# Layer 0's softmax reciprocals: taken of four gathered rows, and spread from HBM with one load per head pair

## The chip, the cores and the metric

The kernel runs on one NeuronCore of a Trainium2 chip. The metric is device time in microseconds (us) from start to end of the program, the median of several runs. A profile of one execution is used beside it. The engines are named as in the profile: PE is TensorE (matmuls), PEld its weight loads, DVE is VectorE, ACT is ScalarE, POOL is GpSimd, SP is SyncE, which here issues nearly all DMAs.

## What is computed

Eight samples of 512 channels by 1024 positions (32x32), float32, pass through two attention layers with residuals. Layer 0 is the one that the change touches:

```python
# layer 0, per sample: group norm over 32 groups, then 8 heads of 64 channels
qkv = einsum('oc,bchw->bohw', qkv_w, h) + qkv_b
attn = softmax(einsum('bhnd,bhmd->bhnm', q, k) / sqrt(64), axis=-1)
o    = einsum('bhnm,bhmd->bhnd', attn, v)
x    = x + einsum('oc,bchw->bohw', proj_w, o) + proj_b
```

Layer 1 has one sample-wide norm and a single head of 512 channels. Softmax is evaluated without subtracting a maximum: exponentials are summed, and the sum's reciprocal is applied after the product with v, to o rather than to the probabilities. For each query position and head, one reciprocal is therefore needed: 8 heads x 1024 positions per sample.

## The kernel before

**Work and stages.** The samples are taken in turn. For each, layer 0 (`layer0`) makes v, then q and k of the odd head pairs, and then runs a loop over 64 attention units; q and k of the even pairs were made ahead. A unit is (pair, g, kt): a pair of heads, a half g of the queries (512 of them), and one of eight blocks of 128 keys. The pairs come in the order 0, 2, 1, 3. For a unit, PE computes the scores (L921) into one of two PSUM buffers, ACT takes the exponential (L778) into a tile `p`, DVE adds `p` to the pair's running sum `acc` (L780, not for kt = 0), and two units later PE multiplies `p` with v (L940) into one of two other PSUM buffers. After the last kt, ACT (L946) and DVE (L947) move the result out to the output tile `os`, and so free that buffer.

**Order.** PE, ACT and DVE run in the order in which the program text issues their work. In the loop, `couple_steps(i)` places the work on sums so many units after the end of a pair; in the following stage a table `hooks` places it after so many steps of the products that make the next sample's q and k (L612, with evacuations at L425, L642, L644). SP issues its DMAs in program order too, each after the waits ahead of it. SBUF tiles come from a pool of 36 tiles of 128x1024; a new tile's first writer waits for the last users of the tile that had the place before. The two PSUM pools "s" and "o" have two buffers each.

**The sums.** When both halves of a pair are done, three DMAs (`fold`, L1039 to L1041) and one DVE addition (`folded`, L1046) bring its two accumulators into one tile. Two pairs make a couple: pairs 0 and 2, then pairs 1 and 3. Ones-matmuls (`sum_couple`, L1054) then write the sums of the couple's four heads into two banks, one per query half, each head's row repeated over 32 partitions. `copy_couple` (L1063, through `held`, L788) copies a bank to an `inv` tile of 128x512. `one_over_couple` (L1066) takes the reciprocal of that whole tile in place and issues eight DMAs (L1072), each copying 32 rows of a head to 32 partitions of the tile `spreads[pair]`, two copies for each head's 64 channels. `held_couple` (L1078) makes ACT read the reciprocals once, for a check on their size. `divide_couple` (L1081, through `divide`, L960) multiplies `os` by the spread reciprocals.

**Where this stands.** The first couple is handled inside the loop, while the units of pairs 1 and 3 run (7 to 18 units after the end of pair 2). The second couple is handled in the stage after the loop, between the products for the next sample's q and k. Right after that stage comes layer 0's projection (`project`, L612 with tiles `ps_p`), whose operands are `os[0][0]` and `os[1][0]` first, then the differences `t_p` made by `combine2` (L1010), and whose PSUM results DVE evacuates at L1183. Its second chunk of channels in each operand belongs to pairs 1 and 3. The last sample (b = 7) has a path of its own (L1116 to L1131) that the change leaves alone, so the couples occur 14 times, twice in each of 7 samples.

**Layer 1.** `sums` (L1550) already does something like the changed code, once a sample: a reciprocal of a 128x256 tile, a store of its four distinct rows to HBM (L1562), and one load that broadcasts the 4 KB row to all 128 partitions (L1564), with this source:

```python
rows.rearrange("n q -> (n q)").unsqueeze(0).to_broadcast([P, 8 * P])
```

Of the kernel before, what the change touches and what calls it, by code (L numbers as in the profile page):

```python
# [37 lines left out]
FP = mybir.dt.float32  # L38
# [8 lines left out]
P = 128  # L47
C = 512
NC = C // P
N = 1024  # L50
NT = N // P
HALF = 512
HD = 64
# [12 lines left out]
def two_attention_blocks(  # L66
# [17 lines left out]
    nc = tc.nc  # L84
    B = x.shape[0]

    const = ctx.enter_context(tc.tile_pool(name="const", bufs=1))
    tpool = ctx.enter_context(tc.tile_pool(name="t", bufs=36))
    wpool = ctx.enter_context(tc.tile_pool(name="w", bufs=3))
    dram = ctx.enter_context(tc.tile_pool(name="dram", bufs=1, space=bass.MemoryType.DRAM))  # L90
    upool = ctx.enter_context(tc.tile_pool(name="u", bufs=5))
    onepool = ctx.enter_context(tc.tile_pool(name="one", bufs=1))
    accpool = ctx.enter_context(tc.tile_pool(name="acc", bufs=2))
# [4 lines left out]
    def banks(tag, name):  # L98
        return psum.tile([P, 2, HALF], FP, tag=tag, name=name)

    def tile2(name):
        return tpool.tile([P, 2, HALF], FP, tag="t", name=name)
# [8 lines left out]
    def piece(ts, cc, half):  # L111

        return ts[cc // 2][half][:, cc % 2, :]
# [52 lines left out]
    ones = const.tile([P, P], FP, tag="ones", name="ones")  # L166
    nc.gpsimd.memset(ones, 1.0)

    extent = const.tile([P, B * 10 + 2], FP, tag="extent", name="extent")
    extents = iter(range(extent.shape[1]))  # L170


# [90 lines left out]
    def next_weight():  # L263

        w = waiting.pop(0)
        if coming:
            name = coming.pop(0)
            waiting.append(Weight(name) if name in stored else load_first(name))
        return w
# [12 lines left out]
    def room(name, n=-1):  # L282

        return spares[n] if spares else banks("s", f"ps_{name}")[:, 0, :]
# [302 lines left out]
    def together(*groups):  # L587

        groups = list(groups)
        spares.clear()  # L590
        while groups:
            for g in list(groups):
                if next(g, g) is g:
                    groups.remove(g)
                else:
                    yield
        spares.clear()

    def at_steps(steps, hooks):

        n = -1
        for n, _ in enumerate(steps):
            for hook in hooks.get(n, []):
                hook()
        assert n >= max(hooks, default=-1)
# [177 lines left out]
    def held(value, name, to=None):  # L783

        if to is None:
            to = onepool.tile([P, HALF], FP, tag="held", name=f"held_{name}")[:, : value.shape[1]]
        n = next(extents)
        nc.scalar.activation(to, value, AF.Identity, accum_out=extent[:, n : n + 1])  # L788
# [20 lines left out]
    def flat(t):  # L809
        return t.rearrange("p h n -> p (h n)")  # L810

    def pairs_qk(w, oc, bs, qs, ks, b):

        for ts, n, bias, name in [(qs, 0, V_BQ0, "q"), (ks, 1, V_BK0, "k")]:
            for i in (oc, oc + 2):
                t = tile2(f"{name}_0_{b}_{i}")
                ts[i] = [t[:, half, :] for half in range(2)]
            yield make_channels(
                w.parts[n], 0, oc, bs, vec[:, bias : bias + NC],
                lambda chunk, half, ts=ts: ts[chunk][half], f"{name}_0_{b}",  # L820
            )
# [65 lines left out]
    def layer0(bs, qs, ks, b, norm_next):  # L887
# [24 lines left out]
        accs, sums, invs, spreads = {}, {}, {}, {}  # L912
# [45 lines left out]
        def divide(pair, g, inv):  # L958
            part = piece(os, pair, g)
            nc.vector.tensor_tensor(part, part, inv, ALU.mult)  # L960
# [45 lines left out]
        def combine2(n, k):  # L1006
            x, y = {
                1: (os[0][1], os[0][0]), 2: (comb["B22"], comb["T1"]), 3: (comb["B22"], os[0][1]), 4: (comb["B21"], comb["T2"])
            }[n]
            nc.vector.tensor_tensor(comb[f"T{n}"][:, k, :], x[:, k, :], y[:, k, :], ALU.subtract)  # L1010
# [21 lines left out]
        couples, folds, ps_couple = [ORDER[:2], ORDER[2:]], {}, []  # L1032

        def fold(pair):


            (a, c), t = (accs[pair, g] for g in range(2)), tile2(f"fold_{b}_{pair}")
            low, high = slice(0, HD), slice(HD, P)
            nc.sync.dma_start(t[low], a[high])  # L1039
            nc.sync.dma_start(t[high], c[low])  # L1040
            nc.sync.dma_start(a[high], c[high])  # L1041
            folds[pair] = t

        def folded(pair):
            a = accs[pair, 0]
            nc.vector.tensor_tensor(a, a, folds.pop(pair), ALU.add)  # L1046

        def sum_couple(couple, banks_of):


            for n, (pair, j) in enumerate((pair, j) for pair in couple for j in range(2)):
                for g, bank in enumerate(banks_of):
                    rows = slice(g * HD, (g + 1) * HD)
                    nc.tensor.matmul(  # L1054
                        bank[n * 32 : (n + 1) * 32, :], ones[rows, :32], accs[pair, 0][rows, j, :],
                        start=True, stop=True,
                    )
            ps_couple[:] = banks_of

        def copy_couple(couple, g):  # L1060
            name = f"{b}_{couple[0]}_{g}"
            invs[g] = accpool.tile([P, HALF], FP, tag="inv", name=f"inv_{name}")
            held(ps_couple[g], f"sum_{name}", invs[g])  # L1063

        def one_over_couple(couple, g):
            nc.vector.reciprocal(invs[g], invs[g])  # L1066
            for n, pair in enumerate(couple):
                if g == 0:
                    spreads[pair] = tile2(f"inv_{b}_{pair}")
                for j in range(2):  # L1070
                    for r in range(2):
                        nc.sync.dma_start(  # L1072
                            spreads[pair][(j * 2 + r) * 32 : (j * 2 + r + 1) * 32, g, :],
                            invs[g][(n * 2 + j) * 32 : (n * 2 + j + 1) * 32, :],
                        )

        def held_couple(g):
            held(invs.pop(g), f"inv_{b}_{g}")  # L1078

        def divide_couple(couple, g):  # L1080
            for pair in couple:  # L1081
                divide(pair, g, spreads[pair][:, g, :])

        def ended(i):

            pair, g, kt = units[i] if 0 <= i < len(units) else (None, None, None)
            return pair if (g, kt) == (1, NT - 1) else None

        def couple_steps(i):
            if ended(i - 1) is not None:  # L1090
                fold(ended(i - 1))
            if ended(i - 5) is not None:
                folded(ended(i - 5))
            couple = couples[0]
            if ended(i - 7) == couple[1]:
                ps_sum = banks("o", f"ps_sum_{b}_{couple[0]}")
                sum_couple(couple, [ps_sum[:, g, :] for g in range(2)])
            for g, (at_copy, at_over, at_held, at_divide) in enumerate([(7, 8, 14, 13), (8, 10, 18, 15)]):
                if ended(i - at_copy) == couple[1]:
                    copy_couple(couple, g)  # L1100
                if ended(i - at_over) == couple[1]:
                    one_over_couple(couple, g)
                if ended(i - at_held) == couple[1]:
                    held_couple(g)
                if ended(i - at_divide) == couple[1]:
                    divide_couple(couple, g)

        last = norm_next is None
        for i in range(2, len(units) + 2):
# [6 lines left out]
            pair, g, kt = units[i - 5] if i >= 5 else (None, None, None)  # L1116
            name = f"0_{b}_{pair}_{g}"
# [8 lines left out]
            pair, g, kt = units[i - 9] if i >= 9 else (None, None, None)  # L1126
            if pair in invs and kt == NT - 1:
                held(invs.pop(pair), f"inv_0_{b}_{pair}_{g}")
            pair, g, kt = units[i - 10] if i >= 10 else (None, None, None)
# [3 lines left out]
        if b == 0:  # L1133
            rows, = throughs
# [3 lines left out]
        if not last:  # L1138


            couple = couples[1]
            hooks = {
                0: [lambda n=n: combine2(n, 0) for n in range(1, 5)],
                1: [lambda: folded(end)],
                3: [
                    lambda: sum_couple(couple, [room("sum", g) for g in range(2)]),
                    lambda: copy_couple(couple, 0), lambda: copy_couple(couple, 1),
                    lambda: one_over_couple(couple, 0),
                ],
                5: [lambda: held_couple(0)],  # L1150
                6: [lambda: one_over_couple(couple, 1)],
                7: [lambda: divide_couple(couple, 0)],
                8: [lambda: held_couple(1)],
                9: [lambda: divide_couple(couple, 1)] + [lambda n=n: combine2(n, 1) for n in range(1, 5)],
            }
            at_steps(
                together(*pairs_qk(next_weight(), 0, combine.parts, qs_next, ks_next, b + 1)), hooks
            )
# [1011 lines left out]
```

## Time and profile before

| | us |
|---|---|
| three runs: median (lowest to highest) | 2839.69 (2839.13 to 2842.56) |
| profiled execution: span, first to last instruction | 2838.1 |
| PE busy, share of the span | 2825.0 (100%) |
| DVE busy | 2124.3 (75%) |
| ACT busy | 1118.0 (39%) |
| DVE reciprocals of 128x512 (L1066), 28 of them | 93.7 |
| DMAs that spread them (L1072), 224 of them, issue to landing each | 2.0 |

The profiled execution's own time is its span of 2838.1 us; the median of the runs is 1.6 us more. Busy times are unions of an engine's instructions. The ends of matmuls are modelled, so that a PE at 100% is not proof that no time is lost; waits are better seen in the distance from one matmul's start to the next one's. In the timeline lines, the first column is the start in us, the second the time from the first start to the last end of a merged row, then engine, line, operation, output and inputs, shapes, the number of instructions, and in brackets the idle time before it with what ended it.

### The profile page before, as it was taken

How to read it: one execution, taken by the hardware profiler on the slowest of the kernel's cores; microseconds unless marked ns; L12 is line 12 of the kernel's file. 1: busy time of each engine (PE TensorE's matmuls, PEld its weight loads, DVE VectorE, ACT ScalarE, POOL GpSimd, SP SyncE). 2: the span in 40 equal slices, each digit the busy share in tenths (PEclk: the TensorE clock that was granted, in tenths of full speed). 3: DMA queues.
4: the chain of work that ended last, by engine and by line, in shares of the span. 5: the costliest groups of instructions: out<-in, count | busy, mean ns of one | idle time of the engine just before them, and what ended most of it. 6: DMA issues, size and time to landing. Idle time of an engine off the chain costs nothing.

```text
span 2838.1 us, 38370 instructions
## 1 busy us (share of the span) xinstructions
PE 2825.0 (100%) x15328; PEld 1518.4 (53%) x15328; DVE 2124.3 (75%) x2891; ACT 1118.0 (39%) x1564; POOL 273.6 (10%) x236
## 2 busy tenths in 40 slices
PE   9999999999999999999999999999999999999999
PEld 5434765347643476435773356733567335673365
DVE  6686696867867678777777777777777777767867
ACT  3462324623256232553325522265232642326432
POOL 0000220003100040000400004000040000400011
PEclk9999999999999999999999999999999999999999
DMA  8512132121322213213132131322213222121001
GB/s 289 179 42 74 58 121 94 42 89 53 111 93 50 86 70 107 80 46 108 56 108 79 40 106 56 108 79 46 100 59 105 79 56 90 63 85 57 8 16 39
DMA packets 81227, 228.90 MB, mean 81 GB/s; under 512 B 20080, under 2 KB 20880, under 8 KB 74640
## 3 DMA queue, kind: packets, MB, share of 16 engines
q1 hardware_dynamic: 76576, 210.61, 23.0%
q10 hardware_dynamic: 4464, 15.76, 1.7%
q8 instruction: 122, 2.00, 0.3%
q14 instruction: 65, 0.53, 0.1%
HBM read 157.35 MB, written 30.70 MB: 66 GB/s over the span
## 4 chain that ended last, share of the span: by engine, by line
PE 91%; DVE 6%; issue 1%; SPq 1%; DMA 0%; ACT 0%; POOL 0%; DVEq 0%; POOLq 0%
PE s L921 16%; PE ps_o L940 15%; PE ps_q L612 10%; PE ps_v L627 7%; PE ps_o L1489 7%; PE ps_p L612 5%; PE ps_l L1325 4%; PE ps_s L1308 4%; PE ps_k L612 3%; PE ps_l_v L627 3%; PE ps_s L1325 3%; PE ps_l_qk L849 3%; PE ps_s_v L870 2%; PE ps_s_two L1619 2%; PE ps_s_qk L842 2%; PE ps_o_v L870 1%
## 5 line engine op out<-in xcount | busy, mean ns | idle before, releaser
L778 ACT ACTIVATE p<-s 128x1024 f32<-128x1024 f32 x512 | 524.0, 1025 | 322.1 <-PE s L921 308.3
L780 DVE TENSOR_TENSOR acc<-acc,p 128x1024 f32<-128x1024 f32 x384 | 469.2, 1222 | 99.4 <-ACT p L778 86.3
L940 PE MATMUL ps_o<-p,v 64*64 64x512 f32 x4096 | 528.6, 589 | 0.0
L940 PEld LDWEIGHTS ps_o<-p,v 64*64 64x64 f32 x4096 | 156.6, 133 | 282.8 <-issue 278.9
L921 PE MATMUL s<-q,k 64*64 64x512 f32 x2304 | 298.5, 591 | 0.0
L921 PE MATMUL s<-c_q,c_k 64*64 64x512 f32 x1792 | 233.0, 590 | 0.0
L339 POOL TENSOR_TENSOR rstd<-rstd,minus_half 128x4 f32<-128x4 f32 (+1 forms) x16 | 19.8, 1239 | 2087.7 <-DVE rstd L338 2087.7
L921 PEld LDWEIGHTS s<-q,k 64*64 64x64 f32 x2304 | 86.3, 133 | 162.6 <-issue 156.6
L1489 PE MATMUL ps_o<-t_p,s_v 128*128 128x512 f32 x384 | 168.2, 594 | 0.0
L921 PEld LDWEIGHTS s<-c_q,c_k 64*64 64x64 f32 x1792 | 67.7, 133 | 126.3 <-issue 114.9
L780 DVE TENSOR_TENSOR acc<-p,p 128x1024 f32<-128x1024 f32 x64 | 77.9, 1217 | 73.5 <-ACT p L778 73.5
L1299 ACT ACTIVATE p<-p,factor 128x512 f32<-128x512 f32 (+1 forms) x112 | 85.3, 780 | 115.7 <-DVE p L1335 91.2
L1313 ACT COPY p<-ps_s 128x512 f32<-128x512 f32 x96 | 53.1, 588 | 177.1 <-PE ps_s L1308 177.1
L1489 PEld LDWEIGHTS ps_o<-t_p,s_v 128*128 128x128 f32 x384 | 72.3, 190 | 91.3 <-issue 89.2
L1335 DVE TENSOR_TENSOR p<-ps_l,p 128x512 f32<-128x512 f32 x136 | 90.0, 683 | 41.0 <-PE ps_l L1325 40.7
L612 PE MATMUL ps_p<-t_p,w_p 128*128 128x512 f32 x256 | 114.8, 597 | 2.4 <-DVE u_p L1183 1.3
L612 PE MATMUL ps_q<-t,w_wqk 128*128 128x512 f32 x256 | 116.0, 597 | 0.0
L425 ACT COPY u_q<-ps_q 128x512 f32<-128x512 f32 x75 | 43.6, 581 | 177.1 <-PE ps_q L612 177.1
L1066 DVE RECIPROCAL inv<-inv 128x512 f32<-128x512 f32 x28 | 93.7, 3346 | 22.9 <-ACT inv L788 22.9
L425 ACT COPY u_v<-ps_v 128x512 f32<-128x512 f32 x48 | 28.1, 586 | 204.9 <-PE ps_v L627 185.9
L1335 DVE TENSOR_TENSOR p<-ps_s,p 128x512 f32<-128x512 f32 x112 | 74.8, 684 | 37.9 <-PE ps_s L1325 37.9
L627 PE MATMUL ps_v<-w_v,t_again 128*128 128x256 f32 x448 | 99.0, 379 | 0.0
(457 smaller groups left out, 4903.5 us busy)
## 6 DMA issues: line engine op xcount, KB each, us to landing
x<-in_x SPq DMA_DIRECT2D x92, 512.0 KB, 6.8
w_qk<-stored_qk SPq DMA_DIRECT2D x14, 1792.0 KB, 7.3
inv<-inv SPq DMA_DIRECT2D x248, 64.0 KB, 2.0
w_wqk<-stored_wqk SPq DMA_DIRECT2D x8, 1792.0 KB, 7.6
fold<-acc SPq DMA_DIRECT2D x56, 256.0 KB, 3.1
w_wvo<-stored_wvo SPq DMA_DIRECT2D x8, 1792.0 KB, 7.5
out<-x SPq DMA_DIRECT2D x28, 512.0 KB, 3.3
w_v<-stored_v SPq DMA_DIRECT2D x7, 1792.0 KB, 7.1
```

What stands on the lines that cost most here:

```text
L612: nc.tensor.matmul(bank, w[a][:, k, c * P : (c + 1) * P], bs[b][:, k, :], start=fresh and k == 0, stop=k == 1, skip_group_check=True,)
L627: nc.tensor.matmul(bank[:, u * 2 * P : (u + 1) * 2 * P], bs[b][:, k, n * P : (n + 1) * P], w[a][:, k, :], start=fresh and u == k == 0, sto ...
L778: nc.scalar.activation(p, s, AF.Exp, scale=factor)
L780: nc.vector.tensor_tensor(acc, first, p, ALU.add)
L921: nc.tensor.matmul(s[cols, j, :], ks[pair][k0 // HALF][rows, k0 % HALF : k0 % HALF + HD], qs[pair][g][rows, :], start=True, stop=True,)
L940: nc.tensor.matmul(o[cols, half, :], vs[kt][rows, c0 : c0 + HD], p[rows, j, :], start=kt == 0, stop=kt == NT - 1,)
L1066: nc.vector.reciprocal(invs[g], invs[g])
L1299: nc.scalar.activation(p, p, AF.Exp, scale=norm.factor)
L1308: nc.tensor.matmul(bank, bs[v][:, k, t * P : (t + 1) * P], q_parts[a][:, k, :], start=a == "A11" and k == 0, stop=k == 1, skip_group_check ...
L1325: nc.tensor.matmul(bank[:, u * 2 * P : (u + 1) * 2 * P], v[y][:, u * P : (u + 1) * P], a[x], start=start and u == 0, stop=True, skip_group ...
L1335: nc.vector.tensor_tensor(at(r, t), bank, at(r, t), ALU.add)
L1489: nc.tensor.matmul(bank, v_parts[kt // 2][a][:, kt % 2, c * P : (c + 1) * P], p_parts[kt // 2][b][:, kt % 2, cols], start=fresh and kt == ...
```

## The change

Each couple's reciprocals are taken once, of the distinct values alone. `copy_couple` now writes both query halves into one 128x1024 tile `sums`. A new step `gather_couple` copies partitions 0, 32, 64 and 96 of it (four heads' rows of 1024) by DMA into a tile `few` of 128x32. `one_over_couple` takes the reciprocal of `few`, stores it to an HBM tile of 4 rows of 1024, and for each pair issues one load that reads the pair's two rows, each 64 times, into the 128 partitions of `spreads[pair]`. `held_couple` reads `few` once. The four multiplications of a couple are each issued alone: in the loop 15, 16, 17 and 18 units after the end of pair 2 (before: two each at 13 and at 15); in the stage after it, pair 1's two after step 8 and pair 3's two after step 9 (before: both pairs' first halves after step 7, the second halves after step 9). The tile of check values `extent` shrinks with the number of `held` calls.

```diff
-    extent = const.tile([P, B * 10 + 2], FP, tag="extent", name="extent")
+    extent = const.tile([P, B * 8 + 4], FP, tag="extent", name="extent")
...
         def copy_couple(couple, g):
-            name = f"{b}_{couple[0]}_{g}"
-            invs[g] = accpool.tile([P, HALF], FP, tag="inv", name=f"inv_{name}")
-            held(ps_couple[g], f"sum_{name}", invs[g])
-
-        def one_over_couple(couple, g):
-            nc.vector.reciprocal(invs[g], invs[g])
+            if g == 0:
+                invs["sums"] = tile2(f"sums_{b}_{couple[0]}")
+            held(ps_couple[g], f"sum_{b}_{couple[0]}_{g}", invs["sums"][:, g, :])
+
+        def gather_couple():
+            few = invs["few"] = const.tile([P, 32], FP, tag="few", name=f"few_{b}")
+            rows = invs.pop("sums")[0:P:32].rearrange("m g q -> m (g q)")
+            nc.sync.dma_start(few, rows.rearrange("m (a c) -> m a c", c=32))
+
+        def one_over_couple(couple):
+            few = invs["few"]
+            nc.vector.reciprocal(few, few)
+            rows = dram.tile([4, N], FP, tag="inv0", name=f"inv_rows_0_{b}_{couple[0]}")
+            nc.sync.dma_start(rows.rearrange("m (a c) -> (m a) c", c=32), few)
             for n, pair in enumerate(couple):
-                if g == 0:
-                    spreads[pair] = tile2(f"inv_{b}_{pair}")
-                for j in range(2):
-                    for r in range(2):
-                        nc.sync.dma_start(
-                            spreads[pair][(j * 2 + r) * 32 : (j * 2 + r + 1) * 32, g, :],
-                            invs[g][(n * 2 + j) * 32 : (n * 2 + j + 1) * 32, :],
-                        )
+                spreads[pair] = tile2(f"inv_{b}_{pair}")
+                nc.sync.dma_start(
+                    flat(spreads[pair]),
+                    rows[2 * n : 2 * n + 2].unsqueeze(1).to_broadcast([2, HD, N]),
+                )
...
-            for g, (at_copy, at_over, at_held, at_divide) in enumerate([(7, 8, 14, 13), (8, 10, 18, 15)]):
+            for at, step in [
+                (7, lambda: copy_couple(couple, 0)), (8, lambda: copy_couple(couple, 1)),
+                (8, gather_couple), (11, lambda: one_over_couple(couple)), (13, held_couple),
+                *[(15 + n, lambda n=n: divide_at(couple[n // 2], n % 2)) for n in range(4)],
+            ]:
...
                 3: [
                     lambda: sum_couple(couple, [room("sum", g) for g in range(2)]),
-                    lambda: copy_couple(couple, 0), lambda: copy_couple(couple, 1),
-                    lambda: one_over_couple(couple, 0),
+                    lambda: copy_couple(couple, 0), lambda: copy_couple(couple, 1), gather_couple,
                 ],
-                5: [lambda: held_couple(0)],
-                6: [lambda: one_over_couple(couple, 1)],
-                7: [lambda: divide_couple(couple, 0)],
-                8: [lambda: held_couple(1)],
-                9: [lambda: divide_couple(couple, 1)] + [lambda n=n: combine2(n, 1) for n in range(1, 5)],
+                5: [lambda: one_over_couple(couple)],
+                7: [held_couple],
+                8: [lambda g=g: divide_at(couple[0], g) for g in range(2)],
+                9: [lambda g=g: divide_at(couple[1], g) for g in range(2)]
+                + [lambda n=n: combine2(n, 1) for n in range(1, 5)],
             }
```

## The prediction

> **What bounds the kernel now.** I read the head of the page first, then the shares of the chain that ended last, then the waits of PE.
>
> ```profile
> span 2838.1 us, 38370 instructions
> ...
> PE 2825.0 (100%) x15328; PEld 1518.4 (53%) x15328; DVE 2124.3 (75%) x2891; ACT 1118.0 (39%) x1564; POOL 273.6 (10%) x236
> ...
> PE 91%; DVE 6%; issue 1%; SPq 1%; DMA 0%; ACT 0%; POOL 0%; DVEq 0%; POOLq 0%
> ...
> L1066 DVE RECIPROCAL inv<-inv 128x512 f32<-128x512 f32 x28 | 93.7, 3346 | 22.9 <-ACT inv L788 22.9
> ```
>
> PE is the bound nearly throughout. DVE has a quarter of the span free, so the 93.7 us of reciprocals are worth only what they now delay on PE. The waits of PE name little (the first two rows in point):
>
> ```profile
> PE ps_l_v L627 <- DVE c_v L563: 2.0, 1, 2.0
> PE ps_p L612 <- DVE u_p L1183: 1.3, 2, 0.7
> ```
>
> As a busy PE can hide lost time, I took the distances between matmul starts. A 128x512 matmul of the projection starts 0.43 us after the one before. In sample 4 the stage around the second couple reads so, first on PE, then on DVE:
>
> ```profile
> 1639.20 7.03 PE L612 MATMUL ps_p<-o,w_p 128*128 128x512 f32 x16
> 1646.94 1.98 PE L612 MATMUL ps_p<-t_p,w_p 128*128 128x512 f32 x4 [0.72 <-DVE u_p L1183]
> ```
>
> ```profile
> 1639.40 0.75 DVE L644 SCALAR_TENSOR_TENSOR k<-ps_k,vec,u_k 128x512 f32<-128x512 f32 x1 [1.50 <-PE ps_k L612]
> 1640.57 0.69 DVE L960 TENSOR_TENSOR o<-o,inv 128x512 f32<-128x512 f32 x1 [0.42 <-DMA inv<-inv]
> 1643.06 0.69 DVE L960 TENSOR_TENSOR o<-o,inv 128x512 f32<-128x512 f32 x1 [1.80 <-DMA inv<-inv]
> ...
> 1646.20 0.69 DVE L1183 TENSOR_TENSOR u_p<-ps_p,u_p 128x512 f32<-128x512 f32 x1
> ```
>
> Sixteen starts from 1639.20 put the first `t_p` matmul at 1646.07; it came at 1646.94, because DVE stood waiting for spread DMAs and evacuated late. With the reloads of weights that follow, sample 4 lost 1.37 us here. The same reading of samples 0 to 6 gives 0.27, 0.24, 0.23, 0.67, 1.37, 0.74 and 1.28: 4.8 us in all. That is all that faster spreading could win here.
>
> [...] the four-row store of layer 1 (L1562) has four increments 1.5 to 1.7 us after its issue, the broadcast to 128 partitions (L1564) sixteen. Which engines they are, no view shows. [...]
>
> ```profile
> 382.36 0.61 SPq L1562 DMA_DIRECT2D inv_rows<-inv  x1
> 384.15 0.34 SPq L1564 DMA_DIRECT2D inv<-inv_rows  x1
> ```
>
> ```profile
> inv<-inv SPq DMA_DIRECT2D x248, 64.0 KB, 2.0
> ...
> inv<-inv_rows SPq DMA_DIRECT2D x8, 512.0 KB, 3.6
> ```
>
> **What the change removes.** Per couple, DVE loses two reciprocals of 3.35 us, ACT one `held` pass of some 0.8 us, SP sixteen issues of some 0.63 us each. All lie beside PE's work. Worth to the end: at most the 4.8 us.
>
> **What it adds.** (1) A gather of 128 pieces of 128 B from four partitions[...]. No row is like it; 2.0 us is the 64 KB spread, and 2.6 us the load of 512 single elements over 16 engines (`c_v`[...]). I take 2.6; the ends are 1.9 and 3.6, the fastest and the slowest landing of a spread. (2) A reciprocal of 128x32. 128x512 takes 3346 ns and 128x256 takes 1750, so 6.2 ns a column and 155 fixed: 0.36 us. (3) A store of 16 KB and the wait for it: layer 1 needs 1.79 us from store to load; for eight short pieces an engine I take 1.95. (4) Two broadcasts of 512 KB, on which all turns. Their size is that of L1564, but not their pattern. L1564's source has 128 as its slowest dimension; in the changed kernel's program the source reads [2 rows][64 times][1024][...]. The packet records of L1564 show 128 packets of 4096 B, 0.159 us each at the median, and the first engine done 2.64 us after issue: 8 x 0.159 = 1.27 of data and 1.36 fixed. With 64 packets an engine the data take 10.2 us and the load lands after 11.5 us. The second load of a couple is on the same two engines behind the first and lands 21.7 us after the first one's issue. Lower bound for the pair: 16 engines, 3.6 us and one more 1.3 us behind it, about 5. Upper bound: the page's share of queue q1, 23.0% of 16 engines' span for 210.61 MB, is 20.2 KB per engine and us, so 13.0 us of data each and 27 us for both.
>
> **Second couple** (sample 4's times). ACT's second copy starts at 1626.11 and takes 0.59, so 1626.70. Gather 1629.3. Reciprocal 1629.65; DVE is free until 1631.43. First load issued at 1631.6. Pair 1 lands at 1643.1, pair 3 at 1653.3. DVE multiplies pair 1's two halves (0.65 each), evacuates k (L644, waiting behind them in DVE's order), then waits for pair 3; its first product is done at 1654.0. On PE, the projection's first operand needs pair 1, and the second chunk of its second operand, the seventh start, due at 1639.20 + 6 x 0.43 = 1641.78, needs pair 3's first product. It starts at 1654.1: **12.3 us lost**. After it PE has 4.3 us of matmuls before the first `t_p`, DVE 4.4 us (a product, four differences, L1183) from the same moment less a product: no further loss. The 1.79 MB load of w_wvo queued behind on SP is delayed too, but its use is some 30 us away.
>
> **First couple** (sample 0's times; exponentials start every 1.716 us).
>
> ```profile
> 178.17 0.59 ACT L788 ACTIVATE inv<-ps_sum 128x512 f32<-128x512 f32 x1
> ...
> 178.97 1.02 ACT L778 ACTIVATE p<-s 128x1024 f32<-128x1024 f32 x1
> ```
>
> The exponential at 178.97 is unit +9 after the end of pair 2. The reciprocal stands after unit +11's addition (184.7), so the first load goes at 187.0; pair 0 lands at 198.5, pair 2 at 208.7. DVE is at pair 0's first product at 191.5 and stands until 198.5, does two additions' worth of work, and stands again until 208.7. Then: product 209.35, an addition 210.55, L947 211.2, pair 2's second product 211.9. The wait lists of the changed program say who is behind: the exponential of unit +26 (from sample 1 on) writes the tile that this last product frees. Due at 208.1, it ends at 212.9; the scores of unit +28, due at 210.4, need its PSUM buffer: 2.5 us lost on PE. DVE then has some eleven additions of 1.22 us, a fold and two evacuations outstanding, until 230.3, while the next stage begins on PE at 223.9 (221.4 + 2.5). There k's first use of an "o" buffer waits for the last L947 (due 229.0, gets it at 230.3: 1.3 us), and its next product for L644 behind four differences (0.5 us); with reloads of weights **4.6 us lost**. If DVE's backlog is absorbed, this is 0; with an extra us of landing it grows by about one, so 0 to 10.
>
> Sum: 7 x (12.3 + 4.6) = 118.3, less 4.8: 113.5 us on the profiled 2838.1, and with the 1.6 us between span and median **2953 us**. From less than this come the new moves that cost nothing: four single products instead of pairs in the loop (same DVE time, due well before the next stage), `held` on a small tile, the shifted places in the tile pool (their new waits are on work that ended 3.7 us or more earlier in the trace of before, those of the products apart).
>
> **Rivals.** *All 16 engines serve the loads* (the pattern is flattened). Pair 3 lands about 5 us after issue, at 1636.7; the point that decides is some 9.4 us (1641.0, one product ahead of PE). Nothing stalls, the 4.8 us vanish: 2835. For it: L1564's 3.6 us for the same bytes; against it: the four increments of L1562. *Two engines per load, but other ones for the second.* Pair 3 lands at 1643.5, its product ends after pair 1's two and L644, at 1645.75: 4.0 us a sample, nothing in the loop: 2838.1 + 28 - 4.8 + 1.6 = 2863. *The loop absorbs its stall*: 7 x 12.3 - 4.8, 2921. *Slower engines* (13.0 us of data a load): pair 3 at 1659, 18 us, and about 10 in the loop: 3033. That the reciprocal is not shortened is excluded by 1750 against 3346 ns.
>
> **Chances.** Two shared engines: 0.80, of which most lies within 2921 and 2990, by the loop's 0 to 10 us; other engines for the second load 0.08; 16 engines 0.07; slower engines 0.05. The range, 2890 to 3000, holds the first case and little else, and leaves the three others out. No run can tell 0.2% (5.7 us) from no change with certainty; by that mark 2835 is mostly "same": faster 0.02, same 0.05, slower 0.93.
>
> **What would show it.** The landing of `inv<-inv_rows` in layer 0: near 11.5 and 21 us, with two increments each. DVE at L960 waiting some 7 and 8 us in the loop, some 6 and 8 us before the projection. PE's wait for `o` L960 at the second operand of `ps_p`, 12 us in each of seven samples; the stalls at `t_p` gone; L1066's 93.7 us down to 5. If both loads land within 9 us, the forecast is wrong in its main step.

## The result, and the profile after

The changed kernel takes 3023.09 us (median; 3019.78 to 3025.67) against 2839.95 us for the kernel before, measured beside it: a ratio of 1.0642, 95% interval 1.0627 to 1.0657. The forecast was 2953 us with a range up to 3000: the direction was right, and so was its main cause, two slow loads on two shared DMA engines; the size was too small. The kernel lost 183 us instead of 113.

From the page of the changed kernel: the head, PE's and the clock's busy tenths, and the shares of the chain that ended last.

```profile
span 3018.0 us, 37987 instructions
...
PE 2872.5 (95%) x15328; PEld 1529.1 (51%) x15328; DVE 2042.6 (68%) x2877; ACT 1102.6 (37%) x1536; POOL 273.7 (9%) x236
...
PEclk9998999989999999999999989999999998999999
...
PE 81%; DMA 12%; DVE 6%; issue 1%; ACT 0%; SPq 0%; POOL 0%; DVEq 0%; ACTq 0%; POOLq 0%
```

DVE and ACT have less to do, as the change intends, but 12% of the chain that ended last is now DMA, where it was 0%: by the page's list by line, 6% are the broadcasts (`inv<-inv_rows`) and 5% the folds (`fold<-acc`). PE's clock row, all nines before, now has four eights: that is a term which the prediction lacks. The reciprocals are now cheap (0.35 us each), and the waits say what came in their place. The line of the reciprocals among the groups (instructions, then busy us and mean ns), then the waits (us in total, times, longest):

```profile
L1074 DVE RECIPROCAL few<-few 128x32 f32<-128x32 f32 x14 | 4.9, 350 | 40.5 <-DMA few<-sums 40.5
```

```profile
DVE o L960 <- DMA inv<-inv_rows: 237.1, 28, 9.4
...
PE ps_p L612 <- DVE o L960: 89.9, 14, 8.0
PE s L921 <- ACT p L778: 39.2, 7, 7.3
PE ps_o L940 <- DVE o L947: 3.3, 1, 3.3
```

DVE waits 28 times for the broadcasts, once for each of the 28 loads. PE waits 14 times before the projection (twice in each of seven samples) and some eight times in the loop. The second couple of sample 0, first PE's projection, then DVE's products (start, us, and in brackets the idle time before):

```profile
255.04 1.02 PE L612 MATMUL ps_p<-o,w_p 128*128 128x512 f32 x2
261.85 3.78 PE L612 MATMUL ps_p<-o,w_p 128*128 128x512 f32 x4 [5.78 <-DVE o L960]
272.50 6.71 PE L612 MATMUL ps_p<-o,w_p 128*128 128x512 f32 x10 [6.87 <-DVE o L960]
```

```profile
261.10 1.29 DVE L960 TENSOR_TENSOR o<-o,inv 128x512 f32<-128x512 f32 x2 [8.54 <-DMA inv<-inv_rows]
262.31 0.74 DVE L644 SCALAR_TENSOR_TENSOR k<-ps_k,vec,u_k 128x512 f32<-128x512 f32 x1
271.75 1.29 DVE L960 TENSOR_TENSOR o<-o,inv 128x512 f32<-128x512 f32 x2 [8.70 <-DMA inv<-inv_rows]
```

This is the chain that the prediction described: pair 1's load, its two products, k's evacuation, pair 3's load. PE's third start waits for the first, its seventh for the second. But look at the durations: four starts from 261.85 take 3.78 us, where four took 1.98 before (1646.94 in the prediction's lines). The same stage by windows (window and its length, then busy us and instructions of PE, PEld, DVE, ACT and POOL, then the granted clock, the share of the DMA engines, GB/s):

```profile
250.00:256.00 6.00, 6.00 (x15) 2.37 (x13) 0.75 (x1) 1.38 (x2) 0.00 (x0) 1.00 0.12 51
256.00:262.00 6.00, 0.22 (x2) 0.15 (x1) 0.90 (x2) 0.00 (x0) 0.00 (x0) 0.82 0.98 278
262.00:265.00 3.00, 3.00 (x4) 1.02 (x4) 1.06 (x2) 0.59 (x1) 0.00 (x0) 0.50 0.28 96
265.00:272.00 7.00, 0.63 (x1) 0.00 (x0) 0.25 (x1) 0.00 (x0) 0.00 (x0) 0.50 0.13 53
272.00:275.00 3.00, 2.50 (x3) 1.18 (x4) 2.96 (x6) 0.00 (x0) 0.00 (x0) 0.50 0.12 53
275.00:278.00 3.00, 3.00 (x6) 1.25 (x5) 2.63 (x4) 0.47 (x1) 0.00 (x0) 0.69 0.01 5
278.00:284.00 6.00, 6.00 (x15) 2.66 (x14) 2.14 (x3) 0.12 (x1) 0.00 (x0) 1.00 0.00 0
```

While PE waits here, its clock falls to half (0.82 in the mean of 256 to 262 us, 0.50 from 262 us on), and the matmuls behind the wait start 0.85 us apart instead of 0.43, until some 276.9 (half clock for 1.9 us of the stretch from 275 to 278 gives its 0.69). PE counts as busy for all of 262 to 265 us at that clock, so the waits alone understate the loss.

And the loop of sample 0, the two stops of DVE, and behind them ACT's exponential (here PE waits 3.3 us for L947, which stands behind DVE's second stop):

```profile
201.28 0.69 DVE L960 TENSOR_TENSOR o<-o,inv 128x512 f32<-128x512 f32 x1 [8.61 <-DMA inv<-inv_rows]
...
211.65 0.69 DVE L960 TENSOR_TENSOR o<-o,inv 128x512 f32<-128x512 f32 x1 [7.94 <-DMA inv<-inv_rows]
```

```profile
214.76 1.03 ACT L778 ACTIVATE p<-s 128x1024 f32<-128x1024 f32 x1 [3.98 <-DVE o L960]
```

The other six samples differ. Sample 1: the issues on SP, the chain that ended last, then ACT and PE:

```profile
560.66 1.17 SPq L1079 DMA_DIRECT2D inv<-inv_rows  x2
561.96 8.24 SPq L1039 DMA_DIRECT2D fold<-acc  x1
...
585.90 0.47 SPq L1041 DMA_DIRECT2D acc<-acc  x1
```

```profile
561.96 23.54 DMA fold<-acc
...
585.90 2.86 DMA acc<-acc
```

```profile
588.83 1.94 ACT L778 ACTIVATE p<-s 128x1024 f32<-128x1024 f32 x2 [8.89 <-DMA acc<-acc]
```

```profile
589.91 1.98 PE L921 MATMUL s<-c_q,c_k 64*64 64x512 f32 x8 [6.83 <-ACT p L778]
```

SP issues the first copy of pair 1's fold (L1039) right behind the two broadcasts. In the kernel before, such a copy landed 2.9 us after its issue (median). Here fourteen of its sixteen increments came after 10.4 to 11.1 us and the last two after 23.3 and 23.5, 1.0 us after pair 2's load had landed on its two engines. L1041 must wait for that copy, and ACT's exponential waits for L1041. In samples 1 to 6 this is the wait that ended PE's stall, and not one for DVE's last product, which was done 0.5 to 1.2 us before L1041 landed (at 587.56 in sample 1).

What the loads themselves do is seen in the DMA view of 187 to 215 us of sample 0 (40 slices), the packets' rate:

```profile
GB/s 20 0 12 12 53 53 35 53 53 53 53 47 47 47 59 228 187 53 64 47 53 47 59 47 129 211 123 53 47 59 47 47 59 47 59 35 12 0 193 181
```

For 24 us the rate stands near 50 GB/s, which is two engines at one packet of 4096 B per 0.16 us; in the windows above, the share of the 16 engines is 0.12 from 250 to 256 us, with both loads of the second couple under way, and 0.12 to 0.13 from 265 to 275 us. The bursts of some 200 GB/s between are the folds' copies. As data land, the trace has two increments for each of the 28 broadcasts, as forecast, and four for each gather. Medians over seven samples of when the loads land, from the couple's first issue on: 13.4 us for pair 0, 23.9 for pair 2, 14.1 for pair 1, 25.2 for pair 3.

Read as distances between matmul starts, the loss in the profiled execution is this: in the loop 43.4 us of waits and 15.1 us of starts at half speed behind them; from the loop's end to the projection 97.5 and 24.8 us. The sum is 180.8; the spans differ by 179.9. The kernel before had lost 4.8 us of its own by the same reading, so some 4 us of the difference are not found.

### The profile page after: what moved, and what is told of

Same layout as the page of the kernel before. It is cut to its first block, busy times and chain, and to the rows that moved or that the text cites. A ratio compares the mean times of both kernels' runs of the same rounds, so it can differ in the third digit from the quotient of the medians.

```text
span 3018.0 us, 37987 instructions
## 1 busy us (share of the span) xinstructions
PE 2872.5 (95%) x15328; PEld 1529.1 (51%) x15328; DVE 2042.6 (68%) x2877; ACT 1102.6 (37%) x1536; POOL 273.7 (9%) x236
## 4 chain that ended last, share of the span: by engine, by line
PE 81%; DMA 12%; DVE 6%; issue 1%; ACT 0%; SPq 0%; POOL 0%; DVEq 0%; ACTq 0%; POOLq 0%
PE s L921 12%; PE ps_o L940 12%; PE ps_q L612 9%; DMA inv<-inv_rows 6%; PE ps_v L627 6%; PE ps_o L1492 6%; PE ps_p L612 6%; DMA fold<-acc 5%; PE ps_l L1328 4%; PE ps_s L1311 4%; PE ps_l_v L627 3%; PE ps_s L1328 3%; PE ps_l_qk L849 2%; PE ps_k L612 2%; PE ps_s_v L870 2%; PE ps_s_two L1622 2%
## 5 line engine op out<-in xcount | busy, mean ns | idle before, releaser
L940 PE MATMUL ps_o<-p,v 64*64 64x512 f32 x4096 | 534.6, 595 | 3.3 <-DVE o L947 3.3
L940 PEld LDWEIGHTS ps_o<-p,v 64*64 64x64 f32 x4096 | 157.7, 135 | 294.0 <-issue 284.2
L921 PE MATMUL s<-c_q,c_k 64*64 64x512 f32 x1792 | 241.6, 611 | 39.2 <-ACT p L778 39.2
L612 PE MATMUL ps_p<-o,w_p 128*128 128x512 f32 x192 | 118.1, 757 | 89.9 <-DVE o L960 89.9
L960 DVE TENSOR_TENSOR o<-o,inv 128x512 f32<-128x512 f32 x64 | 42.6, 688 | 237.1 <-DMA inv<-inv_rows 237.1
L612 PEld LDWEIGHTS ps_p<-o,w_p 128*128 128x128 f32 x192 | 44.5, 241 | 159.7 <-DVE o L960 106.4
L425 ACT COPY u_p<-ps_p 128x512 f32<-128x512 f32 x48 | 28.1, 586 | 242.8 <-PE ps_p L612 216.0
L612 PE MATMUL ps_q<-t,w_wqk 128*128 128x512 f32 x256 | 116.0, 597 | 0.0
L612 PE MATMUL ps_p<-t_p,w_p 128*128 128x512 f32 x256 | 112.6, 592 | 0.5 <-DVE inv L792 0.5
```

Of the source, the lines that this page charges most:

```text
L425: nc.scalar.copy(us[n][:, :width], line[:, :width])
L612: nc.tensor.matmul(bank, w[a][:, k, c * P : (c + 1) * P], bs[b][:, k, :], start=fresh and k == 0, stop=k == 1, skip_group_check=True,)
L921: nc.tensor.matmul(s[cols, j, :], ks[pair][k0 // HALF][rows, k0 % HALF : k0 % HALF + HD], qs[pair][g][rows, :], start=True, stop=True,)
L940: nc.tensor.matmul(o[cols, half, :], vs[kt][rows, c0 : c0 + HD], p[rows, j, :], start=kt == 0, stop=kt == NT - 1,)
```

## The experiments

Theory A is the prediction's, with the clock added: two shared DMA engines land the loads late, and everything lost follows from that. All edits are to the changed kernel, or to a run of it that is named. Each time stands beside a kernel before of 2839.8 to 2840.3 us.

**One row per load.** Each pair's load is split in two, so that a source reads [64 times][1024] and not [2 rows][64 times][1024].

```diff
-                nc.sync.dma_start(
-                    flat(spreads[pair]),
-                    rows[2 * n : 2 * n + 2].unsqueeze(1).to_broadcast([2, HD, N]),
-                )
+                for j in range(2):
+                    nc.sync.dma_start(
+                        flat(spreads[pair])[j * HD : (j + 1) * HD],
+                        rows[2 * n + j : 2 * n + j + 1].to_broadcast([HD, N]),
+                    )
```

> The changed kernel, but each pair's broadcast is issued as two loads, one per row, to 64 partitions each; bytes, packets of 4096 B and everything else unchanged. Theory A (the two-row pattern puts 512 KB on two DMA engines, and all that was lost follows from the late landing): sixteen increments per load, both pairs landed about 5 to 6 us after the first issue, no wait of DVE for the loads over 3 us, no stall of PE, 2835 us (before less the 4.8 us lost at the first t_p matmuls). Rival B (reading the same HBM rows 64 times is what is slow): landings and time as in the changed kernel, near 3020. Rival C (part of the loss is from the other edits: single quotients, moved steps, other places in the tile pool): loads fast, but the time clearly above 2840.

Measured: 2837.13 us, ratio to before 0.9988, interval 0.9981 to 0.9995. Sixteen increments a load; in sample 0 pair 0 landed at 5.0 us and pair 2 at 7.3, pair 1 at 4.6 and pair 3 at 6.8 (a little later than expected, and early enough). The DMA view of 187 to 215 us and DVE's products before the projection:

```profile
GB/s 0 0 140 304 228 211 187 269 240 228 76 64 211 164 193 141 0 0 0 0 0 0 0 0 0 0 0 0 0 0 0 187 187 0 23 0 0 0 0 0
```

```profile
244.36 1.28 DVE L960 TENSOR_TENSOR o<-o,inv 128x512 f32<-128x512 f32 x2
247.12 0.75 DVE L644 SCALAR_TENSOR_TENSOR k<-ps_k,vec,u_k 128x512 f32<-128x512 f32 x1 [1.48 <-PE ps_k L612]
247.79 1.28 DVE L960 TENSOR_TENSOR o<-o,inv 128x512 f32<-128x512 f32 x2
```

The same bytes in the same packets move at some 200 GB/s and are done in less than a third of the time. Of the 56 products five still wait for a load, 6.3 us in all, and no wait of PE follows from them. Rivals B and C fall: the rows are not slow to read, and the other edits cost nothing. This version is also the better one of the three: it beats the kernel before by 0.12% (interval 0.05 to 0.19%).

**One couple at a time.** The split into two one-row loads is made for one couple only; the other couple keeps the two-row loads. The diff is that of the run that mends the loop; the other run asks for `couples[1]`.

```diff
+                if couple == couples[0]:
...
+                else:
```

> Only the first couple (in the loop) gets the two one-row loads; the second couple keeps the two-row loads. Theory A with independent couples: the changed kernel's stalls of the second couple remain, 95 us of waiting of PE and 25 us of matmuls at half speed behind the waits over seven samples, so 2835 + 120 = 2955. Rival D (the loop's delay feeds the second couple's, or the second couple's stall stands in for the loop's): off by more than 10 us from that.

> Only the second couple gets the two one-row loads; the loop's couple keeps the two-row loads. Theory A with independent couples: the loop's stalls remain, 46 us of waiting of PE and 15 us of half-speed matmuls, so 2835 + 61 = 2896. Rival D: off by more than 10 us from that. With the run that mends the loop alone, the two excesses over the run that mends both should add up to the whole loss, about 183 us.

Measured: 2956.33 us with the loop mended, 2897.83 with the second couple mended, that is 119.2 and 60.7 above the run with both mended. PE's waits in these two, in that order:

```profile
PE ps_p L612 <- DVE o L960: 88.4, 14, 7.5
```

```profile
PE s L921 <- ACT p L778: 39.9, 6, 7.5
PE ps_o L940 <- DVE o L947: 4.0, 1, 4.0
```

Each run shows the waits of its own couple only, and the two excesses add up to 179.9 of the 186.0 that separate the changed kernel from the run with both mended. The couples are independent to within 6 us, so rival D falls; the four runs of the changed kernel alone spread over 5.9 us, so these 6 us may be no difference at all.

**Three engines.** A row's 64 partitions are filled by a load of 57 and one of 7.

```diff
+                for lo, hi in ((0, 57), (57, HD)):
+                    for j in range(2):
+                        nc.sync.dma_start(
+                            flat(spreads[pair])[j * HD + lo : j * HD + hi],
+                            rows[2 * n + j : 2 * n + j + 1].to_broadcast([hi - lo, N]),
+                        )
```

> Each row goes to its 64 partitions in two loads, of 57 and of 7 partitions: [...] Theory A puts that load on three engines and the load of 7 on seven. Three increments for a load of 57; 38 packets of about 0.157 us an engine and pair; first pair landed some 8.5 us after its first issue, second pair some 14.5. Nothing stalls in the loop; before the projection PE waits some 0.7 us and 2.7 us, together 3.5 a sample: 2835 + 7 x 3.5 = 2860. If matmuls run at half speed only after waits of 3 us or more, none do; if they do so after any wait of 2 us or more, about 1.9 us a sample more, 2873. Rival B: as the changed kernel, near 3020 (the same bytes and rows), or, if only two-row patterns are slow, 2835.

Measured: 2910.68 us. The increments are as forecast, three for a load of 57 and seven for one of 7, and one-row loads of 57 are slow too: before the packets of w_wvo the DMA view mostly has 74 GB/s, where one-row loads of 64 move some 200. Nothing stalled in the loop. In the second couple of sample 0 the first pair's loads of 57 had landed at 8.6 us and the whole pair at 9.3. The time missed all values, because the second pair's loads of 57 landed at 18.2 us (all of it at 18.9) and not 14.5:

```profile
249.12 1.98 PE L612 MATMUL ps_p<-o,w_p 128*128 128x512 f32 x4 [0.63 <-DVE o L960]
258.73 3.65 PE L612 MATMUL ps_p<-o,w_p 128*128 128x512 f32 x4 [7.62 <-DVE o L960]
```

Of use here: the four starts behind a wait of 0.63 us run at full speed (1.98 us), the four behind 7.62 us at half (3.65). SP also issues the 1792 KB load of w_wvo 8.7 us after the couple's first issue; its packets ran from 9.7 us on, and while they did, the broadcasts' packets took 0.27 us each (median) instead of 0.16. A run further below tests this.

**The half-speed starts.** On top of the run that mends the loop, idle matmuls are put into PE's two waits, into the bank that the real matmul then overwrites.

```diff
-            return strassen(by_channels(w, c, comb), done, f"p_0_{b}_{c}")
+            real = by_channels(w, c, comb)
+
+            def multiply(bank, a, by, fresh):
+                more = {"A11": 6, "A12": 10}.get(a, 0) if c == 0 and not last else 0
+                for _ in range(more):
+                    nc.tensor.matmul(
+                        bank, w[a][:, 0, :P], comb[by][:, 0, :],
+                        start=True, stop=True, skip_group_check=True,
+                    )
+                real(bank, a, by, fresh)
+
+            return strassen(multiply, done, f"p_0_{b}_{c}")
```

> The run that mends the loop's couple alone, plus idle work on PE in seven samples: six extra matmuls (12 starts, 5.2 us) ahead of the projection's first operand and ten (20 starts, 8.6 us) ahead of its second, into the bank that the real one then overwrites. They stand inside PE's two waits for the two-row loads. Theory A with the half-speed term (matmuls behind a wait of several us run at half clock because PE stood idle): no half-speed starts; the first wait shrinks to below 1 us; the second would be 9.4 us without them and is filled; what is won is only the half-speed starts behind the second wait, some 2 us a sample, since those behind the first are hidden in the wait for the second load: 2956 - 14 = 2942. Rival E (the slow starts belong to the late operands or to the loads' traffic, not to PE's idleness): slow starts stay, 2956 or above.

With `"A12": 0` in place of 10:

> The same with the six extra matmuls ahead of the first operand alone. Theory A: the half-speed starts behind the first wait vanish, the second wait grows by as much, because the second load's landing sets its end, and those behind it stay: no change, 2956 within 2 us. Rival F (half-speed starts cost time wherever they stand): some 1.7 us a sample gained, 2944.

Measured: 2940.69 us with both filled, 2955.86 with the first alone, against 2956.33 without. PE with both waits filled, and a window in it, then PE with the first alone (L1214 is the idle work):

```profile
246.70 5.31 PE L1214 MATMUL ps_p<-o,w_p 128*128 128x512 f32 x12
251.85 1.93 PE L612 MATMUL ps_p<-o,w_p 128*128 128x512 f32 x4
253.62 8.75 PE L1214 MATMUL ps_p<-o,w_p 128*128 128x512 f32 x20
...
264.02 4.56 PE L612 MATMUL ps_p<-o,w_p 128*128 128x512 f32 x10 [0.80 <-DVE o L960]
```

```profile
240.00:270.00 30.00, 29.20 (x68) 12.54 (x68) 10.05 (x16) 3.35 (x7) 0.00 (x0) 1.00 0.30 96
```

```profile
251.59 2.94 PE L612 MATMUL ps_p<-o,w_p 128*128 128x512 f32 x6
263.95 6.65 PE L612 MATMUL ps_p<-o,w_p 128*128 128x512 f32 x10 [9.41 <-DVE o L960]
```

With PE kept busy the clock stays at 1.00, ten starts take 4.56 us instead of 6.65 (the run with the first wait alone filled), and 15.6 us come back although PE does more. Rival E falls. Filling the first wait alone gains nothing: the second wait, 7.2 us in sample 0 with neither filled, becomes 9.4 us. Here half-speed starts cost only behind the last wait for the couple's loads, so rival F falls too.

**Another issuing engine.** The loop is mended; the second couple's second load is issued by ACT.

```diff
-                    nc.sync.dma_start(
+                    (nc.scalar if n else nc.sync).dma_start(
```

> The run that mends the loop's couple alone, with the second couple's second load (pair 3) issued by ACT instead of SP. Theory A [...]: the two loads share two engines, both land near 24 us after the first issue, one wait of PE of some 15 us a sample instead of 5.7 and 7.7, the sum about as before: 2950 to 2965. Rival G (another issuing engine brings other DMA engines): both land near 14 us, waits of PE of 5.7 and about 1.5 us, half-speed starts 1.8: 2837 + 7 x 9 = 2900. ACT itself stands at its issue until the store has landed, some 2 us, which may cost up to 1 us a sample in either case.

Measured: 2962.27 us. In sample 1, DVE and PE:

```profile
630.43 1.29 DVE L960 TENSOR_TENSOR o<-o,inv 128x512 f32<-128x512 f32 x2 [18.59 <-DMA inv<-inv_rows]
632.30 1.28 DVE L960 TENSOR_TENSOR o<-o,inv 128x512 f32<-128x512 f32 x2
```

```profile
631.17 9.10 PE L612 MATMUL ps_p<-o,w_p 128*128 128x512 f32 x14 [15.83 <-DVE o L960]
```

Both loads land late, 22 and 24 us after issue (one of the fourteen after 28). In sample 1 the packet records show ACT's load alone for some 3 us, and then both side by side: two packets of the one queue, two of the other, and so on, together at the pace of two engines (one packet per 0.16 us on each). In six of seven samples the two waits of PE become one. Rival G falls.

**Without the weights' traffic.** The load of w_wvo is held back until DVE is done with the couple, first on the run that mends the loop, then on the one with loads of 57.

```diff
-        def __init__(self, name):
+        def __init__(self, name, late=False):
...
+            if late:
+                nc.vector.memset(self.tile[:, :1], 0.0)
             if name in stored:
                 nc.sync.dma_start(self.tile, stored[name])
...
-        w = next_weight().parts[0]
+        w = next_weight(late=not last).parts[0]
         at_steps(together(project(w, 0), project(w, 1)), {})
```

> The run that mends the loop's couple alone, with the 1.79 MB load of w_wvo held back in seven samples until DVE is done with the second couple (DVE writes one column of the weights' tile behind the last difference, so the load that follows must wait). In the other runs it starts some 9.7 us after the second couple's first load and runs on all engines; the broadcasts' packets took 0.24 us in that time instead of 0.17. Theory H (this traffic is why the second pair lands at 25.2 us after the first issue and not near 23): it lands near 23.0, PE's wait before it is 2.2 us shorter a sample: 2956 - 15 = 2941. Rival I (the longer packets cost the two engines nothing, the pace is set elsewhere): 2956. The weights' first use is some 50 us after the couple, so their own lateness should cost nothing; if it does, the time is above this.

> The run with loads of 57 and 7 partitions, with the load of w_wvo held back in the same way. There the last load of 57 landed 18.1 us after the couple's first issue, 3.6 us later than worked out without other traffic. Theory H: it lands near 15, PE's wait before the second operand falls from 7.5 to some 4.5 us a sample, matmuls behind it still run at half speed (1.8 us): 2911 - 21 = 2890. Rival I: 2911.

Measured: 2941.01 us (15.3 less) and 2889.12 us (21.6 less). PE's waits in the two, in that order (both edits add lines, so that L614 and L962 are the L612 and L960 of before):

```profile
PE ps_p L614 <- DVE o L962: 74.7, 14, 7.7
```

```profile
PE ps_p L614 <- DVE o L962: 35.5, 14, 4.4
```

In the first, pair 1 landed at 12.9 us and pair 3 at 23.1 from the first issue (medians; 14.2 and 25.1 in the run with the loop mended, with the weights beside them). In the second, the last load of 57 landed 15.0 us after the first issue in sample 0, and PE's waits fell from 56.9 to 35.5 us. Theory H holds, rival I falls: here the loads on two engines are stretched by traffic that is mostly on the others. In the run with the loop mended, 112 of the 128 packets of w_wvo ran from some 9.7 to 17.4 us after the couple's first issue, and the other 16 only after the broadcasts had landed.

## Why the prediction was right and wrong

**The bound and the mechanism: right.** The pattern [2 rows][64 times][1024] put each broadcast on two engines, both loads on the same two. That such a load gets two engines, and the second load the same two, was the author's assumption; of the traces of before, only the four increments of L1562 beside the sixteen of L1564 bear on it. The runs bear it out: two increments a load, a share of 0.12 of the 16 engines with both loads under way, a second landing 10.5 to 11.1 us behind the first (medians), and with ACT as issuer again the pace of two engines. Loads of 57 had three increments, loads of 64 sixteen. DVE's stops, and the start of the projection that pair 3 holds up, the seventh, came where they were forecast; pair 1 held up the third start as well, so that PE's one forecast wait came as two. In the loop it was otherwise, as told below.

**The small steps: right.** Reciprocal 0.35 us (forecast 0.36); gather 2.0 us (2.6, ends 1.9 and 3.6); store to load 1.46 to 1.78 us, once 2.14 (1.95). In the second couple the first load was issued 8.5 us ahead of the projection's first start, 0.9 us earlier than forecast (7.6). The moves and single products cost nothing, as the run with both couples mended shows.

**What is removed: mostly right.** The stalls at the first `t_p` matmul are gone. The forecast for that case was 2835; the run measured 2837.1. Its profile has 3.2 us less from the first loop to the seventh, against 3.5 forecast for these six samples; some of it is lost again elsewhere (0.7 us before the first loop), which was not followed up.

**The step that failed: "After it PE has 4.3 us of matmuls before the first `t_p` ... no further loss", and its like in the loop.** The prediction counted a stall of PE as the wait alone. In the changed kernel each of the 21 long waits, 3.3 to 8.0 us by the profile, was followed by matmuls at half clock, at the latest 1.3 us after PE had resumed. Its waits of 1.4 us (L612, sample 0) and 2.0 us (L627, last sample) were not: the clock is 1.00 from 234 to 242 and from 2912 to 2920 us. Over ten runs the wait at L627 was followed by it in three. In the second couple of sample 0 the clock is 0.50 behind the waits and 1.00 again from 278 us on. The profile of before, whose longest wait of PE is that at L627 (2.0 us) and whose mean clock is 1.000, does not show this, and the prediction had no term for it. In the second couple this is worth 15.6 us over seven samples (the run with both waits filled). In the loop the distances give 15.1 us; that part was read and not tested by a run of its own.

**Mis-sized: the landing of the loads.** Forecast 11.5 and 21.7 us from the first issue, in both couples; measured 13.4 and 23.9 in the loop, 14.1 and 25.2 before the projection. The data term was right (0.16 us a packet and, without the weights beside them, 10.2 us between the two landings). Two things were left out. Other DMAs slowed the two engines: the load of w_wvo costs 15.3 us over seven samples in the second couple, by the run that holds it back. And the first packets of a couple's loads took 0.2 to 1.3 us each. Folds run beside the loop's loads; what that costs these loads was not tried.

The second couple adds up: 119.2 us measured, of which 7 x 12.3 = 86.1 are the forecast wait, 15.6 the half clock, 15.3 the weights' traffic, and 2.2 are left. That the 12.3 us fit so well is in part luck: without the weights' traffic the loads still landed 1.4 us later than forecast, and the issue 0.9 us earlier nearly made up for it (in that run the seventh start of sample 0, due at 248.7, came at 261.49, 12.8 us late).

**The path that it had wrong: PE's wait in the loop.** The loop was forecast at 7 x 4.6 = 32 us; it cost 60.7. In sample 0 PE's waits were near the forecast in size: 3.3 us in the loop (forecast 2.5 at the scores; here it stood at L940, behind L947), and 1.4 and 0.6 at the start of the next stage (1.3 and 0.5). In the other six PE waited 5.9 to 7.3 us in the loop and not in the next stage, and there the wait that ended last was the one that the prediction lacks: the fold's copy, whose last pieces stood behind the broadcasts on the two engines (landed 0.6 to 1.0 us after pair 2's load). The prediction had applied that order to the couple's second load and to w_wvo, but not to the folds. Of the 60.7 us some 15 are half clock; the rest is 13.4 us more than forecast, by later landings and by the fold. The runs that mend the loop's loads land this copy early too (5.8 us after its issue in sample 0 with both mended), so they show that the loads are the cause of the 60.7 us, but not what the fold's share is: that stays open. The stated 0 to 10 us a sample held, by its size and not by its path: 8.7.

**The range** took these losses as uncertain only through the loop's 0 to 10 us and left the second couple's 12.3 us fixed; its upper end needed the second couple's traffic and clock. The rival "slower engines", at 3033 us, comes close in time but not in cause: without other traffic the packets were as fast as forecast (0.16 us at the median).

## What to carry to other kernels

Read from a trace what a broadcast's pattern gets, in increments and in GB/s, before sizing it: here [2][64][1024] had two increments and some 50 GB/s, two loads of [64][1024] sixteen each and some 200 GB/s, and that was worth 186 us of a kernel. When a forecast stall leaves PE idle as long as the waits here (3.3 us and more), add the half-speed matmuls behind it, but only behind the last wait of a chain: to fill the first of two alone gave 0.5 us. The loads on two engines were slowed by the traffic beside them (pair 3 landed at 25.1 us with w_wvo and at 23.1 without), and a copy with sixteen increments that was issued behind them was done only after them (23.1 to 24.4 us after its issue instead of 2.9). So look up what SP issues next, and who waits for that.

## What was not expected of the hardware

- PE's granted clock was 0.50 behind the waits of 3.3 us and more, and waits filled with idle matmuls were followed by full speed (1.00): 15.6 us back over seven samples, while filling only the first of two waits for one chain of loads gave 0.5 us.
- The loads on two engines suffered from traffic that was mostly on the others: in the changed kernel the broadcasts' packets took 0.23 us instead of 0.17 us on the average while 14,336 B packets of another load ran.
- Two such loads issued by two different engines took turns, two packets of the one queue and two of the other: they landed at 22 and 24 us, where issued one after the other by SP they landed at 14 and 25.
- A copy with sixteen increments, issued right behind the two loads, landed 23.1 to 24.4 us after its issue in seven samples (median before: 2.9), though fourteen of its sixteen increments were there within 12 us.
